# Attention over 4096 positions in split fp32: moving three SBUF tiles by 64 bytes and widening two row pitches from 258 to 260 floats

## The chip, the cores and the metric

The kernel runs on one core of one Trainium2 chip. The metric is device time in microseconds (us) of one execution, taken as the median of several runs. A core has a matrix engine (PE in the profile, with its weight loads shown apart as PEld), a vector engine (DVE), an activation engine (ACT), GpSimd (POOL) and SyncE (SP). They work from an on-chip memory of 128 partitions (SBUF), and PE writes to accumulators (PSUM). A matmul multiplies a stationary operand, which a weight load (LDWEIGHTS) brings into the array, with a moving operand, which the MATMUL streams through it. Both are read from SBUF.

## The reference

For each of four images x of shape 64 x 64 x 256, with N = 4096 positions and C = 256 channels, the reference makes q and k (128 wide) and v (256 wide) by projection, an N x N table of energies, its softmax, and the weighted sum of v:

```python
q = x @ Wq + bq ; k = x @ Wk + bk ; v = x @ Wv + bv
pq = q.reshape(B, -1, N); pk = k.reshape(B, -1, N); pv = v.reshape(B, -1, N)
energy = einsum('bcn,bcm->bnm', pq, pk)
attention = softmax(energy, axis=-1)
out = einsum('bcm,bnm->bcn', pv, attention)
out = gamma * out.reshape(x.shape) + x
```

The reshape runs over the flat memory of an image, so "channels" and "positions" of the attention are not those of the convolution layout; the kernel handles that with the way it loads its rows.

## The kernel before

PE multiplies in a fast form of fp32 (fp32r) that drops low bits. To keep accuracy, every factor is held in three forms: h (an upper part), l and d (two combinations of the rest with the upper part). A product then takes three matmuls. This holds for the energies (forms of q and k side by side in the tiles `q` and `k`) and for the weighted sum (tiles `h`, `l`, `d` of the exponentials against `vh`, `vl`, `vd` of v).

`vh` and `vl` are [128 partitions, 32 blocks m, 258 floats]: 256 of v and two columns of ones (L208), so that the sum of the exponentials falls out of the same matmul. `vd` is [128, 32, 256]. The three stay in SBUF for a whole image. `h`, `l` and `d` are [128, 4, 256] each, in pools with three, two and two buffers.

An image first goes through 16 projection rounds (transposes L123, `qk` L136, `v` L157, then the forms are made on ACT and DVE). Then come 128 steps u, eight (t = 0 to 7) for each of 16 groups g of 256 output rows, so 512 steps over four images. In one step PE does this, in the order the program gives by hand:

- `energy` (L303): 12 matmuls for the step three ahead. Stationary is a 128 x 128 slice of `k`, moving a 256-wide slice of `q`. ACT takes the exponentials (L307) and DVE multiplies their two halves (`join`, L317).
- `attend` (L351), called for j = 0 and 1: 12 matmuls each, four with `vh` and `h`, four with `vl` and `l`, four with `vd` and `d`. Stationary is `left[:, i, n]`, 512 bytes for each partition; moving is row m of `vh`, `vl` or `vd`, with m = 2t + i//2 + 16*(i%2). So i = 0 and 1 read rows with even m, i = 2 and 3 rows with odd m.

DVE makes `l` (L328) and `d` (L331) one step ahead. At the end of a group `whole` and `finish` scale, transpose (`ot`, L389), add x and write the output with a DMA from POOL's queue (L394).

After the last image a check runs: `ok`, a [128, 128] tile in the pool `const`, is made on DVE from the row sums `zall` (L474 to L476), reduced to `zs` (L477), summed over partitions by a matmul (`zp`, L480), and cast to `again` (L481). All engines load `again` and branch on it (L488); a general version of the kernel follows behind that branch and does not run with this data.

SBUF is given out in the order of the pools: `const`, then `xpool` (x tiles), `xtpool`, `qkv` (the v forms), `ppool` (x, y, h, l, d), `work`, `kpool`.

Of the kernel before, what the change touches and what calls it, by code (L numbers as in the profile page):

```python
# [9 lines left out]
F32 = mybir.dt.float32  # L10
F32R = mybir.dt.float32r
I32 = mybir.dt.int32
AF = mybir.ActivationFunctionType
ALU = mybir.AluOpType
AX = mybir.AxisListType
# [5 lines left out]
def kernel(  # L21
# [36 lines left out]
    nc = tc.nc  # L58
    B, W, H, C = x.shape
    P = 128  # L60
    N = W * H
    C2 = C // 2
    NM = N // P
    KC = C // P
    NI = NM // 2
    Z_LOW, Z_HIGH = 2.0**-60, 2.0**80
# [11 lines left out]
    const = ctx.enter_context(tc.tile_pool(name="const", bufs=1))  # L78
# [8 lines left out]
    ones = const.tile([P, P], F32, name="ones")  # L87
# [87 lines left out]
    NJ = NB // P  # L175
    NG = N // NB
    NU = NM // 4
    STEPS = NG * NU
    LOOK = 3
    E = 2.0**-12  # L180


# [5 lines left out]
    bv4_sb = const.tile([P, KC], F32, name="bv4_sb")  # L188
    nc.scalar.mul(bv4_sb, bv_sb, 1.0 / E)

    with ExitStack() as fast:
        fast.enter_context(tc.manual_schedule())
        pool = lambda name, bufs, **kw: fast.enter_context(
            tc.tile_pool(name=name, bufs=bufs, **kw)
        )
        xpool, xtpool, qkv = pool("xpool", 3), pool("xtpool", 3), pool("qkv", 1)
        ppool, work, kpool = pool("ppool", 2), pool("work", 2), pool("kpool", 3)
        dram = pool("dram", 2, space=DRAM)
        ps_s = pool("ps_s", 2, space=PSUM)
# [1 line left out]
        ps_t = pool("ps_t", 1, space=PSUM)  # L201


        vh = qkv.tile([P, NM, C + 2], F32R, tag="vh", name="vh")
        vl = qkv.tile([P, NM, C + 2], F32R, tag="vl", name="vl")
        vd = qkv.tile([P, NM, C], F32R, tag="vd", name="vd")
        for t in (vh, vl):
            nc.vector.tensor_copy(t[:, :, C:], ones[:, : 2 * NM].rearrange("p (m t) -> p m t", t=2))  # L208

        images, qd, kf, units, loads, now = [], {}, {}, {}, {}, {}  # L210

# [13 lines left out]
        def image(b):  # L225
# [7 lines left out]
            def v_out(i):  # L233
                now["v4"] = work.tile([P, KC, C], F32, tag="v4", name=f"v4_{b}_{i}")
                return now["v4"], bv4_sb, 1.0 / E

# [7 lines left out]
        def halved(f, x):  # L244

            h = f[:, :, 0, :]
            nc.scalar.activation(h, x, AF.Identity, scale=UPPER / 64)  # L247
            for j, s, op in ((1, -64.0, ALU.add), (2, 64.0 * (1.0 + E), ALU.subtract)):
                nc.vector.scalar_tensor_tensor(
# [12 lines left out]
        def project_v(b, i):  # L262
# [3 lines left out]
            h = vh[:, m, :C]  # L266
            nc.scalar.activation(h, v4, AF.Identity, scale=UPPER * E)  # L267

            for t, f in ((vl, 1.0 / E), (vd, 1.0 / E + 1.0)):
                nc.vector.scalar_tensor_tensor(  # L270
# [19 lines left out]
        def energy(b, u, k):  # L290
# [10 lines left out]
            for i in range(2):  # L301
                for to, f, first, last in ((sa, 0, True, False), (sa, 1, False, True), (sb, 2, True, True)):
                    nc.tensor.matmul(  # L303
                        to[:, i], kt[:, 2 * k + i, f, :], q[:, :, f, :], start=first, stop=last
                    )
            for to, sp, scale in ((x, sa, (1.0 + E) / E), (y, sb, -1.0 / E)):
                nc.scalar.activation(  # L307
# [28 lines left out]
        def attend(b, u, j):  # L336
            g, t = divmod(u, NU)
            if t == j == 0:
                now["acc"] = [
                    ps_o.tile([P, C + 2], F32, tag=f"a{j}", name=f"a{j}_{b}_{g}")  # L340
                    for j in range(NJ)
                ]
                now["bb"] = ps_o.tile([P, NJ, C], F32, tag="bb", name=f"bb_{b}_{g}")
            h, l, d = units[b, u]
            a, bb = now["acc"][j], now["bb"]
            n = slice(j * P, (j + 1) * P)
            for out_, left, right in ((a, h, vh), (a, l, vl), (bb[:, j, :], d, vd)):
                for i in range(4):
                    m = 2 * t + i // 2 + NI * (i % 2)

                    nc.tensor.matmul(  # L351
                        out_,
                        left[:, i, n],
                        right[:, m, :],
                        start=(t == i == 0 and (left is h or left is d and j == 0)),
                        stop=(t == NU - 1 and i == 3 and left is not h),
                        skip_group_check=True,
                    )
            if t == NU - 1 and j == NJ - 1:
                now["o"] = work.tile([P, NJ, C], F32, tag="o", name=f"o_{b}_{g}")  # L360
                nc.scalar.copy(now["o"], bb)
# [51 lines left out]
        for b in range(B):  # L413
# [17 lines left out]
            for u in range(STEPS):  # L431
                g, t = divmod(u, NU)
                ahead = u + LOOK
                if ahead // NU + 1 < NG and ahead % NU == 3:
# [23 lines left out]
                for j in range(NJ):  # L458
                    attend(b, u, j)
# [10 lines left out]

    zs = const.tile([P, 1], F32, name="zs")
    zf = zall.rearrange("p n j -> p (n j)")
    ok = const.tile([P, B * NG * NJ], F32, name="ok")
    nc.vector.tensor_scalar(ok, zf, Z_LOW, None, ALU.is_ge)  # L474
    nc.vector.scalar_tensor_tensor(ok, zf, Z_HIGH, ok, ALU.is_le, ALU.mult)
    nc.vector.tensor_reduce(zs, ok, AX.X, ALU.min)  # L476
    nc.vector.tensor_scalar(zs, zs, 0.5, None, ALU.is_lt)  # L477
    with tc.tile_pool(name="ps_z", bufs=1, space=PSUM) as ps_z:
        zp = ps_z.tile([P, 1], F32, name="zp")
# [4 lines left out]
    NG = N // NB  # L484
    NJ = NB // P
    NP = NM // 2
    xg, og = columns(x, NB), columns(out, NB)
    with tc.If(nc.values_load(again[0:1, 0:1]) > 0), ExitStack() as general:  # L488
        pool = lambda name, bufs, **kw: general.enter_context(
            tc.tile_pool(name=name, bufs=bufs, **kw)  # L490
        )
        xpool, xtpool, qkv = pool("gx", 2), pool("gxt", 2), pool("gqkv", 1)
# [4 lines left out]
        for b in range(B):  # L497
# [16 lines left out]
            for g in range(NG):  # L514
                ps = []
                mx = work.tile([P, 2, NB], F32, tag="mx", name=f"gmx_{b}_{g}")
                for t in range(NP):
# [9 lines left out]
                    p = ppool.tile([P, 2, NB], F32, tag="p", name=f"gp_{b}_{g}_{t}")  # L527
# [89 lines left out]
```

## Time and profile before

| what | value |
|---|---|
| median of 4 runs | 2520.83 us (2519.0 to 2521.51) |
| the profiled execution's own time | 2522.84 us |
| its span, first to last instruction | 2520.7 us |
| granted TensorE clock, mean over the span | 0.997 |
| busy share PE / PEld / DVE / ACT / POOL | 99% / 97% / 83% / 72% / 17% |
| matmuls L351 (`vh`, `vl`, `vd`), each | 4096 of 285, 283, 281 ns |
| matmuls L303 (`sa`, `sb`) | 4096 of 280 ns, 2048 of 281 ns |
| `x`, `l`, `d` on DVE, 512 each | 1222, 1219, 1219 ns |
| mean rate of DMA | 198 GB/s |

Matmuls overlap in the array, so the mean duration of one (some 280 ns) is not what it costs. What counts is the step from the start of one to the start of the next, which a timeline shows.

### The profile page before, as it was taken

How to read it: one execution, taken by the hardware profiler on the slowest of the kernel's cores; microseconds unless marked ns; L12 is line 12 of the kernel's file. 1: busy time of each engine (PE TensorE's matmuls, PEld its weight loads, DVE VectorE, ACT ScalarE, POOL GpSimd, SP SyncE). 2: the span in 40 equal slices, each digit the busy share in tenths (PEclk: the TensorE clock that was granted, in tenths of full speed). 3: DMA queues.
4: the chain of work that ended last, by engine and by line, in shares of the span. 5: the costliest groups of instructions: out<-in, count | busy, mean ns of one | idle time of the engine just before them, and what ended most of it. 6: DMA issues, size and time to landing. Idle time of an engine off the chain costs nothing.

```text
span 2520.7 us, 49987 instructions
## 1 busy us (share of the span) xinstructions
PE 2486.9 (99%) x19970; PEld 2440.3 (97%) x19970; DVE 2103.8 (83%) x2440; ACT 1805.4 (72%) x3138; POOL 424.8 (17%) x774
## 2 busy tenths in 40 slices
PE   8999999999999999999999999999999999999998
PEld 7999999999899999999989999999998999999998
DVE  4888888888688888888868888888876888888886
ACT  4777777777577777777667777777766777777775
POOL 3211111111311111111041111111114111111110
PEclk9999999999999999999999999999999999999999
DMA  6666666664766666656476666666547666666663
GB/s 213 207 209 198 206 196 194 207 206 155 223 211 193 209 199 207 199 190 208 141 240 211 199 195 209 200 206 197 190 148 235 210 207 192 205 200 206 199 198 98
DMA packets 137967, 498.92 MB, mean 198 GB/s; under 512 B 15872, under 2 KB 57856, under 8 KB 137728
## 3 DMA queue, kind: packets, MB, share of 16 engines
q0 software_dynamic: 92160, 453.03, 56.0%
q1 hardware_dynamic: 44032, 41.96, 5.5%
q8 instruction: 160, 2.62, 0.4%
q10 hardware_dynamic: 1536, 0.66, 0.1%
q14 instruction: 79, 0.65, 0.1%
HBM read 445.25 MB, written 50.33 MB: 197 GB/s over the span
## 4 chain that ended last, share of the span: by engine, by line
PE 90%; issue 3%; ACT 3%; DVE 2%; DMA 1%; POOL 0%; POOLq 0%; ACTq 0%; DVEq 0%
PE a L351 38%; PE bb L351 19%; PE sa L303 18%; PE sb L303 10%; PE qk L136 2%; PE v L157 1%; ACT v L166 1%; DMA k<-kf 1%; PE ot L389 1%; ACT vh L267 1%; DVE qks L145 1%; ACT f L247 1%; DVE vd L270 0%; PE xt L123 0%; DMA bv_sb<-in_L_conv_bv_dram 0%
## 5 line engine op out<-in xcount | busy, mean ns | idle before, releaser
L307 ACT ACTIVATE x<-sa 128x512 f32<-128x512 f32 x1024 | 608.3, 594 | 430.7 <-PE sa L303 421.4
L317 DVE TENSOR_TENSOR x<-x,y 128x1024 f32<-128x1024 f32 x512 | 625.7, 1222 | 164.9 <-ACT y L307 164.9
L303 PE MATMUL sa<-q,k 128*128 128x256 f32 x4096 | 744.7, 280 | 9.1 <-DMA k<-kf 5.1
L351 PE MATMUL a<-vh,h 128*128 128x258 f32 x4096 | 666.7, 285 | 0.0
L351 PE MATMUL a<-vl,l 128*128 128x258 f32 x4096 | 659.7, 283 | 1.7 <-DVE l L328 1.7
L351 PE MATMUL bb<-vd,d 128*128 128x256 f32 x4096 | 650.7, 281 | 1.8 <-DVE d L331 1.8
L303 PEld LDWEIGHTS sa<-q,k 128*128 128x128 f32 x4096 | 623.0, 189 | 11.3 <-ACT x L307 5.0
L331 DVE SCALAR_TENSOR_TENSOR d<-h,x 128x1024 fp32r<-128x1024 f32 x512 | 624.0, 1219 | 0.0
L328 DVE TENSOR_TENSOR l<-x,h 128x1024 fp32r<-128x1024 f32 x512 | 624.0, 1219 | 0.0
L307 ACT ACTIVATE y<-sb 128x512 f32<-128x512 f32 x1024 | 612.5, 598 | 0.0
L303 PE MATMUL sb<-q,k 128*128 128x256 f32 x2048 | 576.4, 281 | 0.0
L351 PEld LDWEIGHTS a<-vl,l 128*128 128x128 f32 x4096 | 563.1, 189 | 2.6 <-DVE l L328 2.6
L322 ACT ACTIVATE h<-x 128x1024 fp32r<-128x1024 f32 x512 | 543.4, 1061 | 29.4 <-DVE x L317 29.4
L351 PEld LDWEIGHTS a<-vh,h 128*128 128x128 f32 x4096 | 560.4, 190 | 1.3
L351 PEld LDWEIGHTS bb<-vd,d 128*128 128x128 f32 x4096 | 556.5, 188 | 2.6 <-issue 2.0
L287 POOL DMA_DIRECT2D k<-kf x512 | 283.3, 554 | 1487.1 <-PE sb L303 1467.0
L303 PEld LDWEIGHTS sb<-q,k 128*128 128x128 f32 x2048 | 384.5, 188 | 8.5 <-ACT y L307 1.0
L136 PE MATMUL qk<-wqk_sb,xts 128*128 128x256 f32 x512 | 124.6, 387 | 5.1 <-ACT xts L129 5.1
L157 PE MATMUL v<-xts,wv_sb 128*128 128x256 f32 x512 | 120.3, 379 | 0.0
L381 ACT ACTIVATE o<-o,r 128x256 f32<-128x256 f32 x128 | 58.4, 504 | 74.0 <-DVE r L379 74.0
L157 PEld LDWEIGHTS v<-xts,wv_sb 128*128 128x128 f32 x512 | 97.4, 190 | 13.3
L136 PEld LDWEIGHTS qk<-wqk_sb,xts 128*128 128x128 f32 x512 | 94.6, 195 | 16.2 <-ACT xts L129 5.5
(41 smaller groups left out, 876.7 us busy)
## 6 DMA issues: line engine op xcount, KB each, us to landing
k<-kf POOLq DMA_DIRECT2D x512, 768.0 KB, 4.7
x<-in_x_dram SPq DMA_DIRECT2D x128, 256.0 KB, 3.3
kf<-f POOLq DMA_DIRECT2D x64, 384.0 KB, 3.7
out_dram<-x POOLq DMA_DIRECT2D x64, 256.0 KB, 2.5
qd<-qks POOLq DMA_DIRECT2D x128, 64.0 KB, 2.2
qr<-qd SPq DMA_DIRECT2D x64, 128.0 KB, 3.1
wv_sb<-in_L_conv_Wv_dram ACTq DMA_DIRECT2D x1, 256.0 KB, 4.2
wqk_sb<-in_L_conv_Wq_dram ACTq DMA_DIRECT2D x1, 128.0 KB, 2.1
```

What stands on the lines that cost most here:

```text
L136: nc.tensor.matmul(qk[:, s, :], self.xt[i][:, k, s, :], wqk_sb[:, k, :], start=(k == 0), stop=(k == KC - 1),)
L145: nc.vector.tensor_tensor(dst, qk[:, :, o : o + w], bqk_sb[:, o : o + w].unsqueeze(1).to_broadcast([P, 2, w]), ALU.add,)
L157: nc.tensor.matmul(vp[:, eh, :], wv_sb[:, k, eh * P : (eh + 1) * P], self.xt[i][:, k].rearrange("p s a -> p (s a)"), start=(k == 0), stop= ...
L287: nc.gpsimd.dma_start(t.rearrange("p (i s) f d -> p i s (f d)", s=2), kf[b, u % NU])
L303: nc.tensor.matmul(to[:, i], kt[:, 2 * k + i, f, :], q[:, :, f, :], start=first, stop=last)
L307: nc.scalar.activation(to[:, 2 * k : 2 * k + 2, :], sp.rearrange("p i j d -> p i (j d)"), AF.Exp, scale=scale,)
L317: nc.vector.tensor_tensor(x, x, y, ALU.mult)
L322: nc.scalar.activation(h, units[b, u], AF.Identity, scale=UPPER)
L328: nc.vector.tensor_tensor(l, x, h.bitcast(F32), ALU.subtract)
L331: nc.vector.scalar_tensor_tensor(d, h.bitcast(F32), 1.0 + E, x, ALU.mult, ALU.subtract)
L351: nc.tensor.matmul(out_, left[:, i, n], right[:, m, :], start=(t == i == 0 and (left is h or left is d and j == 0)), stop=(t == NU - 1 and ...
L381: nc.scalar.activation(o[:, j, :], o[:, j, :], AF.Identity, scale=r[:, j : j + 1])
```

## The change

The tile `pad` of [128, 16] floats (64 bytes for each partition) is allocated behind `qkv` and never used. The rows of `vh` and `vl` are VC = 260 floats apart (1040 bytes) where they were 258 (1032 bytes); the ones still fill columns 256 and 257, and the matmul reads as many columns as its output has (258). To make room, `ok` leaves `const` for a pool `check` that is opened after the main pools are closed, and so lies where x tiles lay.

```diff
+    VC = C + 4
...
         xpool, xtpool, qkv = pool("xpool", 3), pool("xtpool", 3), pool("qkv", 1)
+
+        pool("pad", 1).tile([P, 16], F32, name="pad")
         ppool, work, kpool = pool("ppool", 2), pool("work", 2), pool("kpool", 3)
...
-        vh = qkv.tile([P, NM, C + 2], F32R, tag="vh", name="vh")
-        vl = qkv.tile([P, NM, C + 2], F32R, tag="vl", name="vl")
+        vh = qkv.tile([P, NM, VC], F32R, tag="vh", name="vh")
+        vl = qkv.tile([P, NM, VC], F32R, tag="vl", name="vl")
...
-            nc.vector.tensor_copy(t[:, :, C:], ones[:, : 2 * NM].rearrange("p (m t) -> p m t", t=2))
+            nc.vector.tensor_copy(t[:, :, C : C + 2], ones[:, : 2 * NM].rearrange("p (m t) -> p m t", t=2))
...
-                        right[:, m, :],
+                        right[:, m, : out_.shape[1]],
...
-    ok = const.tile([P, B * NG * NJ], F32, name="ok")
-    nc.vector.tensor_scalar(ok, zf, Z_LOW, None, ALU.is_ge)
-    nc.vector.scalar_tensor_tensor(ok, zf, Z_HIGH, ok, ALU.is_le, ALU.mult)
-    nc.vector.tensor_reduce(zs, ok, AX.X, ALU.min)
+    with tc.tile_pool(name="check", bufs=1) as check:
+        ok = check.tile([P, B * NG * NJ], F32, name="ok")
+        nc.vector.tensor_scalar(ok, zf, Z_LOW, None, ALU.is_ge)
+        nc.vector.scalar_tensor_tensor(ok, zf, Z_HIGH, ok, ALU.is_le, ALU.mult)
+        nc.vector.tensor_reduce(zs, ok, AX.X, ALU.min)
```

Where the tiles lie (byte address in a partition, first buffer) in the two built programs:

| tile | before | after |
|---|---|---|
| `vh`, first row | 36128 | 35616 |
| `vl`, first row | 69152 | 68896 |
| `vd`, first row | 102176 | 102176 |
| `h` / `l` / `d` | 155424 / 167712 / 175904 | 155488 / 167776 / 175968 |
| `q` / `k` | 194336 / 210784 | 194400 / 210848 |
| `ok` | 23328 | 23328, the first 512 bytes of an x buffer |
| end of the last tile | 229216 | 229280 |

## The prediction

> **What bounds the kernel now.** I read the shares of the page first, then the chain of waits, then the timeline of single steps.
>
> ```profile
> PE 2486.9 (99%) x19970; PEld 2440.3 (97%) x19970; DVE 2103.8 (83%) x2440; ACT 1805.4 (72%) x3138; POOL 424.8 (17%) x774
> ...
> PE a L351 38%; PE bb L351 19%; PE sa L303 18%; PE sb L303 10%; PE qk L136 2%; PE v L157 1%; ACT v L166 1%; DMA k<-kf 1%; PE ot L389 1%; ACT vh L267 1%; DVE qks L145 1%; ACT f L247 1%; DVE vd L270 0%; PE xt L123 0%; DMA bv_sb<-in_L_conv_bv_dram 0%
> ```
>
> PE is never free, and 85% of the chain is L351 and L303. So the end is set by how fast matmuls follow each other. The timeline of PE in the middle of the run shows that, step by step (start, length, engine and line, tiles):
>
> ```profile
> 1002.02 0.39 PE L303 MATMUL sa<-q,k 128*128 128x256 f32 x2
> ...
> 1003.38 0.64 PE L351 MATMUL a<-vh,h 128*128 128x258 f32 x4
> 1003.85 0.64 PE L351 MATMUL a<-vl,l 128*128 128x258 f32 x4
> 1004.33 0.64 PE L351 MATMUL bb<-vd,d 128*128 128x256 f32 x4
> 1004.81 0.64 PE L351 MATMUL a<-vh,h 128*128 128x258 f32 x4
> 1005.29 0.64 PE L351 MATMUL a<-vl,l 128*128 128x258 f32 x4
> 1005.77 0.64 PE L351 MATMUL bb<-vd,d 128*128 128x256 f32 x4
> 1006.25 0.40 PE L303 MATMUL sa<-q,k 128*128 128x256 f32 x2
> ...
> 1028.18 0.40 PE L303 MATMUL sa<-q,k 128*128 128x256 f32 x2
> ...
> 1029.59 0.66 PE L351 MATMUL a<-vh,h 128*128 128x258 f32 x4
> ```
>
> The reader is to see three speeds. Twelve energies take 1003.38 - 1002.02 = 1.36 us, 113.3 ns each; 24 attend matmuls take 1006.25 - 1003.38 = 2.87 us, 119.6 ns each; and in another step twelve energies take 1029.59 - 1028.18 = 1.41 us, 117.5 ns each. Nobody is waited for in any of them. From the start times of all matmuls in the trace I took the step to the next start, leaving out steps over 150 ns: energies have two values and little between, 60% near 113.4 ns and 40% near 117.7, mean 115.3. The others are, on rows of even m and of odd m: `vh` 119.9 and 121.9, `vl` 119.4 and 121.0, `vd` 117.5 and 118.5 ns. Two more columns explain 0.8 ns of the first two (256 columns at 113.4 ns is 0.44 ns each). A step repeats to 1 ns from group to group, so the cause isn't a chance meeting with another engine; it lies in PE's own two reads, whose addresses repeat.
>
> The sum closes: 12288 attend steps at 120.9, 120.2 and 118.0 are 1471 us; 6144 energies at 115.3 are 708; 1024 projection matmuls at 216 and 512 transposes at 109 are 277; steps over 150 ns add 39; the time before the first matmul of line 136 is 11.6, the end after the last of line 351 some 12.6. That is 2519 of the span of 2520.7. The execution's own time, 2522.84, is 2.1 over the span and 2.0 over the median of the runs, so I take differences off the median.
>
> The end of the program matters too:
>
> ```profile
> 2508.00 0.23 DVE L474 TENSOR_SCALAR ok<-zall 128x128 f32<-128x128 f32 x1
> ...
> 2509.72 0.14 DVE L481 CAST again<-zp 128x1 int32<-128x1 f32 x1
> ...
> 2512.82 0.70 POOL L394 DMA_DIRECT2D out_dram<-x  x1 [26.31 <-DVE x L393]
> ```
>
> The check of the row sums is done (2509.86) before the last output leaves (2512.82).
>
> **The change part by part.** *d against vd.* The distance of `d` from `vd` goes from 73728 bytes, a multiple of 128, to 73792, which leaves 64. All rows of `vd` and slices of `d` are multiples of 512 apart, so every one of the 4096 pairs of `bb` changes alike. The trace has one pair of operands that already lies 64 apart: `k` from `q` is 16448 bytes, which leaves 64 by 128, also after the change. It runs at 115.3 ns, `bb` at 118.0. From below: the shift does nothing, 0 us. From above: every `bb` falls to the faster energy value, 4096 x (118.0 - 113.4) = 19 us. I take the energies' mean, as theirs is the nearest row: 4096 x 2.7 = 11 us gained. A loss can't be excluded: all at the slowest kind of step (121.9 less two columns, 121.0) would cost 12 us.
>
> *Rows of vh and vl.* At 1032 bytes rows of odd m begin 8 bytes off a multiple of 16, and the distance to `h` and `l` runs through 8m by 128; at 1040 every row begins on a multiple of 16 and the distance is 64 - 16m. Odd rows are slower by 2.0 (`vh`) and 1.6 ns (`vl`); but `vd`, whose rows are all aligned, has 1.0 for the same places in the program. Taking all of it away gains 2048 x (2.0 + 1.6) = 7.3 us, taking what is over `vd` 2048 x 1.6 = 3.3. I take 7. The 64 bytes do less here: in the trace of before the even rows already sit at distances 0, 16, ... 112 as t goes from 0 to 7, and `vh` reads 119.4, 119.6, 122.1, 120.0, 119.6, 119.5, 119.8, 119.0 ns: nothing good about 64 (t = 4). Ends: every pair at the faster energy value plus two columns (114.2) gains 4096 x (120.9 - 114.2) + 4096 x (120.2 - 114.2) = 52 us; all at the worst of these places (122.1) loses 4096 x (1.2 + 1.9) = 13.
>
> *The energies.* Their distances stay. Which of two values they run at depends on what ran before, since the same tiles give both. All fast gains 6144 x 0.4 x 4.3 = 10.6 us, all slow loses 16. I take 0.
>
> These steps of 113.4 to 121.9 ns, with a pattern that repeats by row at a granted clock of 0.997, are what all three gains rest on. The Trainium skill speaks against them: "TensorE: Matmul & The Clock Gate", Part 2, "Step-by-step: what each phase is for", says that weights and moving operand come through two independent read ports, so that loading the next weights takes nothing from the running matmul. By that page no address matters and the sum would hold the end alone, 2526 us as an estimate. Rows that differ by address under one instruction contradict it, and I go by the rows.
>
> *The check at the end.* `ok` moves into memory of the x tiles, so its first instruction waits until the pool is free, which is when the last output DMA has landed; in the built order it stands behind that output's addition (L393 before). Queued behind it are `zs`, `zp`, `again`, and the load and branch of all five engines. Before, these were hidden under `finish`. The DMA's end is seen at 2516.14 in the trace; from `ok` to `again` is 2509.86 - 2508.00 = 1.86 us; so `again` comes at 2518.0. Before, POOL's load began at 2512.81, and its closing drain ran from 2513.54 for 6.35 us, the last long piece. If it lasts as long again, everything moves by 2518.0 - 2512.8 = 5.2 us. If it was mostly waiting for the DMA, PE's branch (3.69 us in the trace) is next: 2518.0 + 0.6 + 3.7 + 0.9 = 2523.2, 2.5 us late. I take 5, the drain being the row itself.
>
> *Free.* `pad` has no instruction. The ones are as many elements. DVE and ACT keep their counts; DVE needs 3 x 1.22 = 3.66 us of a step of 4.26, so PE could lose 0.6 us of a step (300 us in all) before DVE became the bound.
>
> Sum: -11 - 7 + 0 + 5 = -13, so 2520.8 - 13 = 2508 us.
>
> **The rivals.** *The big gain:* the reads of weights and moving rows collide because both began on the same 128-byte offset, and the steady 113.4 of the energies is what a shifted pair gives. Then `bb` gains 19 and `vh`, `vl` half or all of 52: 2520.8 - 19 - 26 + 5 = 2481, down to 2455. For it: energies hold the low value over twelve matmuls in a row, `bb` never does. Against: distance 64 shows nothing in `vh`.
>
> *Nothing but the rows and the end:* the shift is empty, and 118 for `bb` comes from accumulating in one place or from the order. Then -7 + 5, 2519 us, no change. For it: `vh` by distance; energies have 117.7 too.
>
> *Slower:* a step of the array depends on the state that the step before left, as the two values of the energies show. The new pattern of rows leaves the energies at the slow value from their first matmul on, all through a group: +16 us, the end +5, rows -7: 2535. It decides once the rows give less than 16 + 5. With no gain and no loss in the array the end alone gives 2526.
>
> *It doesn't do what it says:* the addresses of the built program show the shift, so I give this nothing.
>
> **How the numbers follow.** A difference under 0.2% (5 us, 2515.8 to 2525.8) can't be told from none. Forecast (gain in `bb` and rows, less the end): 0.42, its own range 2498 to 2515. Big gain: 0.20. Rows and end alone: 0.15. Slower: 0.23, half of it near 2526. The range 2478 to 2530 leaves out the deep part of the big gain and the full slow energies, about 2 in 10. Faster 0.62, same 0.15, slower 0.23.
>
> **What would show it.** In the profile after: 24 attend matmuls in about 2.82 us where they took 2.87; `bb` steps near 115 ns with the energies' two values; odd and even rows of `vh` alike. `ok` on DVE after the last output DMA, and some 5 us more between the last matmul of the weighted sum and the end. I am wrong if `bb` stays at 118, if the energies change their mix, or if the end is no longer than before.

## The result, and the profile after

The changed kernel takes 2523.04 us (median of 40 runs, 2521.2 to 2524.96), the kernel before 2520.36 us in the same comparison (60 runs). The ratio is 1.0011, 95% interval 1.0007 to 1.0016: slower by 2.7 us, less than the 0.2% that the prediction called no change, and on the other side of the forecast of 2508.

The first lines of the page are nearly those of before. Line numbers have moved by 3: L306 is `energy`, L354 `attend`.

```profile
PE 2483.7 (99%) x19970; PEld 2436.8 (97%) x19970; DVE 2104.1 (83%) x2440; ACT 1811.2 (72%) x3138; POOL 426.4 (17%) x774
...
L354 PE MATMUL a<-vl,l 128*128 128x258 f32 x4096 | 659.3, 283 | 1.7 <-DVE l L331 1.7
L354 PE MATMUL a<-vh,h 128*128 128x258 f32 x4096 | 659.9, 283 | 0.0
L354 PE MATMUL bb<-vd,d 128*128 128x256 f32 x4096 | 649.0, 280 | 1.9 <-DVE d L334 1.9
```

PE still sets the end. `vh` has lost 2 ns of mean duration (285 before), `bb` one (281), `vl` none. The timeline of PE in the same part of the run (start, length, engine and line, tiles) shows what follows from it:

```profile
1005.72 0.40 PE L306 MATMUL sa<-q,k 128*128 128x256 f32 x2
...
1007.12 0.64 PE L354 MATMUL a<-vh,h 128*128 128x258 f32 x4
1007.59 0.65 PE L354 MATMUL a<-vl,l 128*128 128x258 f32 x4
1008.07 0.64 PE L354 MATMUL bb<-vd,d 128*128 128x256 f32 x4
1008.55 0.64 PE L354 MATMUL a<-vh,h 128*128 128x258 f32 x4
...
1009.98 0.40 PE L306 MATMUL sa<-q,k 128*128 128x256 f32 x2
```

24 attend matmuls take 1009.98 - 1007.12 = 2.86 us, 119.2 ns each; the twelve energies ahead of them take 1.40 us, 116.7 each, between the two values of before. Over the whole trace, with the measure of the prediction (from the start of a matmul to the next start, steps over 150 ns left out):

| step, ns | before | after | times | us |
|---|---|---|---|---|
| `vh`, rows of even m | 119.90 | 120.05 | 2048 | +0.3 |
| `vh`, rows of odd m | 121.87 | 118.54 | 2048 | -6.8 |
| `vl`, rows of even m | 119.44 | 120.39 | 2048 | +1.9 |
| `vl`, rows of odd m | 121.04 | 119.99 | 2048 | -2.2 |
| `bb` (`vd`) | 118.02 | 117.74 | 4096 | -1.1 |
| energies | 115.34 | 116.24 | 6144 | +5.5 |
| share of energies at the slow value | 40% | 58% | | |

That is -2.4 us in the array. The last matmul of line 351 started at 2507.96 us before; its like now starts at 2504.04, so the trace is ahead by 3.9 us there. The other 1.5 us lie outside these rows, in the projection rounds (steps of `qk` -1.7, waits ahead of the transposes of x -1.3) and in the energies' steps over 150 ns (+1.3); one profiled execution of each kernel can't tell whether the change has any part in them. Then comes the end:

```profile
2503.80 0.52 PE L354 MATMUL bb<-vd,d 128*128 128x256 f32 x3
...
2508.62 0.70 POOL L397 DMA_DIRECT2D out_dram<-x  x1 [25.89 <-DVE x L396]
2511.26 0.23 DVE L478 TENSOR_SCALAR ok<-zall 128x128 f32<-128x128 f32 x1 [2.94 <-DMA out_dram<-x]
...
2513.06 0.16 DVE L485 CAST again<-zp 128x1 int32<-128x1 f32 x1 [0.74 <-PE zp L484]
```

`ok` waits 2.94 us for the last output to land, and `again` is ready at 2513.22, 4.6 us behind the issue of that output, where it was 3 us ahead of it before. From the start of the last `bb` to the end of the span it is 17.13 us, before 12.76: +4.4 us. Together -2.4 + 4.4 = +2.0, against the 2.7 of the medians. The span grew by 0.5 us only, thanks to that 1.5 us; the profiled execution of the kernel before took 2522.84 us, 2.5 over the median here, that of the changed kernel 2523.29, 0.3 over. The steps themselves repeat better than that: e1 and e4 below give those of before and of after again to 0.1 ns by kind.

So three things need an explanation: why `bb` did not gain from the 64 bytes, why the energies got slower though their distance is the same, and what the rows did.

### The profile page after: what moved, and what is told of

It is laid out like the page before. It is cut to its first block, busy times and chain, and to the rows that moved or that the text cites. A ratio compares the mean times of both kernels' runs of the same rounds, so it can differ in the third digit from the quotient of the medians.

```text
span 2521.2 us, 49989 instructions
## 1 busy us (share of the span) xinstructions
PE 2483.7 (99%) x19970; PEld 2436.8 (97%) x19970; DVE 2104.1 (83%) x2440; ACT 1811.2 (72%) x3138; POOL 426.4 (17%) x774
## 4 chain that ended last, share of the span: by engine, by line
PE 91%; ACT 3%; DVE 3%; issue 2%; DMA 1%; POOL 0%; DVEq 0%; POOLq 0%; ACTq 0%
PE a L354 39%; PE bb L354 19%; PE sa L306 19%; PE sb L306 10%; PE qk L136 2%; PE v L157 1%; ACT v L166 1%; PE ot L392 1%; ACT vh L270 1%; DVE qks L145 1%; DMA k<-kf 1%; DVE vd L273 1%; ACT f L250 1%; PE xt L123 0%; DMA bv_sb<-in_L_conv_bv_dram 0%
## 5 line engine op out<-in xcount | busy, mean ns | idle before, releaser
L306 PE MATMUL sa<-q,k 128*128 128x256 f32 x4096 | 750.4, 281 | 8.0 <-ACT x L310 4.0
L354 PE MATMUL a<-vl,l 128*128 128x258 f32 x4096 | 659.3, 283 | 1.7 <-DVE l L331 1.7
L354 PE MATMUL a<-vh,h 128*128 128x258 f32 x4096 | 659.9, 283 | 0.0
L354 PE MATMUL bb<-vd,d 128*128 128x256 f32 x4096 | 649.0, 280 | 1.9 <-DVE d L334 1.9
L306 PEld LDWEIGHTS sa<-q,k 128*128 128x128 f32 x4096 | 626.1, 189 | 10.2 <-ACT x L310 5.0
L306 PE MATMUL sb<-q,k 128*128 128x256 f32 x2048 | 578.1, 282 | 0.0
L354 PEld LDWEIGHTS a<-vl,l 128*128 128x128 f32 x4096 | 562.7, 190 | 2.6 <-DVE l L331 2.6
L354 PEld LDWEIGHTS bb<-vd,d 128*128 128x128 f32 x4096 | 557.9, 189 | 2.6 <-issue 2.0
L354 PEld LDWEIGHTS a<-vh,h 128*128 128x128 f32 x4096 | 557.0, 189 | 0.9
L306 PEld LDWEIGHTS sb<-q,k 128*128 128x128 f32 x2048 | 384.9, 188 | 9.9 <-ACT y L310 8.2
```

The source lines that it names most:

```text
L306: nc.tensor.matmul(to[:, i], kt[:, 2 * k + i, f, :], q[:, :, f, :], start=first, stop=last)
L354: nc.tensor.matmul(out_, left[:, i, n], right[:, m, : out_.shape[1]], start=(t == i == 0 and (left is h or left is d and j == 0)), stop=(t ...
```

## The experiments

"Distance" is always the address of the stationary operand less that of the moving one, modulo 128 bytes. All steps in ns, measured as above; the slow share is the share of energy steps nearer to 117.7 than to 113.4 ns; "end" is the time from the start of the last `bb` to the end of the span, in us; the ratio is to the kernel before, with its 95% interval, where there were repeated runs ("one run" marks the others).

| run | `vh` | `vl` | `bb` | energies | slow share | end | time, us | ratio |
|---|---|---|---|---|---|---|---|---|
| before | 120.90 | 120.24 | 118.02 | 115.34 | 0.40 | 12.8 | 2520.4 | |
| after | 119.28 | 120.19 | 117.74 | 116.24 | 0.58 | 17.1 | 2523.0 | 1.0011 (1.0007 to 1.0016) |
| e1_end_only | 120.93 | 120.30 | 118.00 | 115.30 | 0.39 | 17.5 | 2526.4 | 1.0018 (1.0009 to 1.0027) |
| e2_pad_only | 121.08 | 120.06 | 117.29 | 116.57 | 0.68 | 12.6 | 2528.4 | 1.0028 (1.0017 to 1.0039) |
| e3_rows_only | 120.26 | 119.77 | 119.11 | 116.08 | 0.59 | 12.8 | 2523.4 | 1.0008 (0.9999 to 1.0017) |
| e4_change_early_end | 119.30 | 120.21 | 117.70 | 116.20 | 0.58 | 12.5 | 2520.2 | 0.9997 (0.9988 to 1.0006) |
| e5_qk_moved | 120.87 | 119.96 | 118.21 | 115.94 | 0.45 | 12.8 | 2522.1 | one run |
| e6_k_plus32 | 120.56 | 120.55 | 118.46 | 117.81 | | 12.9 | 2534.5 | one run |
| e7_k_plus64 | 120.58 | 120.17 | 117.98 | 118.92 | | 12.9 | 2536.0 | one run |
| e8_k_plus96 | 120.62 | 119.72 | 118.18 | 119.33 | | 12.9 | 2537.2 | one run |
| e9_grouped_after | 119.50 | 119.91 | 116.51 | 116.99 | 0.80 | 13.0 | 2519.6 | 0.9995 (0.9985 to 1.0004) |
| e10_grouped_before | 120.31 | 120.11 | 118.62 | 117.74 | 0.94 | 12.8 | 2538.1 | 1.0068 (1.0051 to 1.0084) |
| e11_vh_rows_1152 | 119.76 | 120.08 | 117.48 | 117.05 | 0.81 | 12.7 | 2527.9 | 1.0029 (1.0017 to 1.0042) |
| e12_256_dist64 | 115.80 | 113.66 | 114.13 | 117.49 | 0.89 | 12.8 | 2476.3 | one run |
| e13_256_dist0 | 119.94 | 119.99 | 119.73 | 117.98 | 0.99 | 12.8 | 2537.4 | one run |
| e14_260_columns | 120.11 | 119.57 | 116.22 | 117.42 | 0.89 | 13.0 | 2521.3 | 1.0002 (0.9992 to 1.0012) |
| e15_qk_pad_grouped | 120.19 | 119.55 | 115.79 | 117.62 | 0.90 | 13.0 | 2520.0 | 0.9995 (0.9986 to 1.0004) |
| e16_256_all64 | 117.24 | 116.10 | 116.47 | 116.48 | 0.65 | 12.8 | 2496.6 | one run |
| e17_qk_pad_order_kept | 118.96 | 119.59 | 116.98 | 117.83 | 0.96 | 12.5 | 2519.9 | 0.9993 (0.9984 to 1.0002) |
| e18_256_order_kept | 115.75 | 113.51 | 113.99 | 117.48 | 0.89 | 12.5 | 2474.5 | one run |

The median of the kernel before was between 2521.3 and 2522.1 us in the comparisons of e1 to e18.

### The parts of the change alone

**e1_end_only**: the kernel before, with `ok` moved as in the change.

```diff
-    ok = const.tile([P, B * NG * NJ], F32, name="ok")
+    with tc.tile_pool(name="check", bufs=1) as check:
+        ok = check.tile([P, B * NG * NJ], F32, name="ok")
...
```

> Only the tile of the last check is moved, as in the change: it lies in memory of the x tiles. The layout of all matmul operands is that of before, moved as a whole by 512 bytes. My theory: the array runs as before (vh 120.9, vl 120.2, bb 118.0, energies 115.3 ns a step), and the end after the last matmul of the weighted sum grows from 12.7 to some 17 us, so the whole is 4 to 5 us over before (ratio 1.0017). Rival (the end's cost lies in the layout, or is hidden by closing work): the whole is within 1 us of before.

The array is that of before to 0.1 ns in every kind, the end is 17.5 us (+4.7), the whole 5.1 us slower by the medians (ratio 1.0018, that is 2 to 7 us). Its timeline has the same order as that of the changed kernel:

```profile
2506.42 0.63 PE L351 MATMUL bb<-vd,d 128*128 128x256 f32 x4
...
2514.34 0.23 DVE L475 TENSOR_SCALAR ok<-zall 128x128 f32<-128x128 f32 x1 [2.93 <-DMA out_dram<-x]
```

The rival falls: moving the tile costs what the end showed, and nothing hides it.

**e2_pad_only**: the kernel before with the tile `pad`, which fits without moving `ok`.

```diff
+        pool("pad", 1).tile([P, 16], F32, name="pad")
```

> Only the 64 bytes are added behind the v forms; rows stay 258 floats apart and the last check stays early. Shift theory (distance of 64 between d and vd helps): bb falls from 118.0 towards 115.3 ns, 5 to 11 us faster. State theory (the shift only gives the array other meeting points, without a direction): bb stays within 1 ns of 118, the energies' share of slow steps moves somewhere from 40%, the whole is within 6 us of before. If the energies' loss in the changed kernel comes from their own addresses (q and k moved by 64), the slow share rises to some 58% here too.

`bb` falls by 0.7 ns, 3 us, and the energies rise by 1.2 ns, 7.6 us, with 68% of them slow. The shift alone costs 0.28%. Both theories missed the size of that loss; the shift theory's 5 to 11 us are not there. The share that the expectation's last sentence foresaw was passed (68% for 58%), but e5 and e3 speak against its reason.

**e3_rows_only**: rows of 260 floats, no pad. The last check works without a tile: the minimum and the maximum of the row sums are compared with the bounds.

```diff
+    VC = C + 4
...
+    nc.vector.tensor_reduce(zs[:, 0:1], zf, AX.X, ALU.min)
+    nc.vector.tensor_reduce(zs[:, 1:2], zf, AX.X, ALU.max)
+    nc.vector.tensor_scalar(zs[:, 0:1], zs[:, 0:1], Z_LOW, None, ALU.is_ge)
+    nc.vector.scalar_tensor_tensor(zs[:, 0:1], zs[:, 1:2], Z_HIGH, zs[:, 0:1], ALU.is_le, ALU.mult)
```

> Only the rows of vh and vl are 260 floats apart; no pad. The last check works with a minimum and a maximum of the row sums and needs no tile, so it stays early. Alignment theory: odd rows of vh fall from 121.9 to about 118.5 ns, and of vl from 121.0 to about 120, 4 to 7 us, and bb stays at 118.0; the whole is 2 to 7 us faster, less what the energies' mix gives or takes. Rival (odd rows gained by the shift, not by the alignment): odd rows of vh stay near 122.

Odd rows of `vh` fall to 120.5 only (118.5 with the pad), odd rows of `vl` to 120.6: `vh` and `vl` give 4.5 us. But `bb` rises by 1.1 ns and the energies by 0.7, though `vd`, `d`, `q` and `k` all lie where they lay before: 4.5 + 4.5 us lost. Here two kinds of matmul lose what their neighbours gain, with no change of their own. Neither theory said so.

**e4_change_early_end**: the change whole, with that form of the last check.

> The changed layout whole (pad and rows), with the last check early, by a minimum and a maximum. My theory: steps as in the changed kernel (vh 119.3, vl 120.2, bb 117.7, energies 116.2), the end back at 12.7 us: 4 to 5 us under the changed kernel, 1 to 3 us under before (ratio 0.9993). Rival (the check costs nothing): as the changed kernel, 2 to 3 us over before.

Every step is that of the changed kernel, and the end is 12.5 us. Here `again` is ready ahead of the last output again:

```profile
2507.11 0.14 DVE L485 CAST again<-zp 128x1 int32<-128x1 f32 x1
...
2510.00 0.70 POOL L397 DMA_DIRECT2D out_dram<-x  x1 [25.91 <-DVE x L396]
```

Its ratio, 0.9997, lies under the changed kernel's 1.0011 and the intervals don't meet; against before it can't be told from no change. So the layout is worth somewhere between 3 us gained and 1.5 lost, and the moved check costs more than the layout gives.

### What sets an energy's step

**e5_qk_moved** puts the 64 bytes behind the tiles of the exponentials, so only q and k move, together.

```diff
-        ppool, work, kpool = pool("ppool", 2), pool("work", 2), pool("kpool", 3)
+        ppool = pool("ppool", 2)
+        pool("pad", 1).tile([P, 16], F32, name="pad")
+        work, kpool = pool("work", 2), pool("kpool", 3)
```

> The 64 bytes of the change lie behind the tiles of the exponentials instead of ahead of them: q and k move by 64 together, everything that the attend matmuls read stays where it was before. State theory (which of its two values an energy takes is left behind by the attend matmuls ahead of it, and not set by its own addresses): the energies stay at 115.3 ns with 40% slow, attend steps as before, the array's sum within 2 us of 2218. Rival (q's and k's own place makes the energies of the changed kernel slower): slow share near 58%, energies at 116.2 ns.

A share of 45% (115.9 ns) is nearer to the 40% of before than to the 58% and 68% of the runs in which `h`, `l` and `d` moved, though the array's sum rises by some 3 us where the expectation allowed 2. But the mean hides that the energies are slow at other places than before: in the steps t = 1, 5 and 7 of a group, where it was t = 2 and 3. Attend pairs and energy pairs have kept their distances; what has changed is the border, the first k against the last row of `vd` and the first `h` against the last q. In e3 nothing of q and k moved and the share was 59%. So the energies' own addresses don't set the value alone; what runs ahead has a part in it. Whether the border has is asked further down.

**e6_k_plus32, e7_k_plus64, e8_k_plus96** move k alone, by a pad of 8, 16 or 24 floats ahead of `kpool` (shown for e6). Then an energy's distance is 96, 0 or 32 instead of 64.

```diff
+        pool("pad", 1).tile([P, 8], F32, name="pad")
         kpool = pool("kpool", 3)
```

> k alone moves by 32 bytes: its distance from q goes from 64 to 96 (by 128); attend operands stay. Energies run twelve in a row at one distance, so their steady values show what a distance does. Distance theory: one steady value that depends on it, lower than 113.4 or higher than 117.7 ns somewhere among the three distances 96, 0 and 32. State theory: two steady values again at every distance, only the share changes.

> k alone moves by 64 bytes: distance 0 from q, which is the distance that d had from vd before. Distance theory: energies rise to the 118 of bb before. State theory: two values near 113.4 and 117.7 again, share anywhere.

> k alone moves by 96 bytes: distance 32 from q. Distance theory: a steady value of its own, as said for a distance of 96. State theory: two values near 113.4 and 117.7 again, share anywhere.

The distance theory holds in the mean: 117.8 ns at 96, 118.9 at 0, 119.3 at 32, against 115.3 at 64. Its steady value doesn't appear, nor do the two values of the state theory: steps spread from 112 to 127 ns. Distance 32 is no better than 0, so that equal offsets are the bad case is not shown. Twelve energies of e7:

```profile
1005.88 0.40 PE L305 MATMUL sa<-q,k 128*128 128x256 f32 x2
...
1007.30 0.64 PE L353 MATMUL a<-vh,h 128*128 128x258 f32 x4
```

1.42 us, 118.3 ns each, where the fast step of before had 1.36. So the kernel before already had its energies at the best of the four distances, and the reading in the prediction that 64 is a good distance was right. Then why not for `bb`?

### Why bb gained nothing

**e9_grouped_after and e10_grouped_before** give `attend` another order: both j for `vh`, both for `vl`, both for `vd`, so each kind runs eight in a row. e9 has the change's layout with the early check, e10 the layout of before.

```diff
-            for out_, left, right in ((a, h, vh), (a, l, vl), (bb[:, j, :], d, vd)):
-                for i in range(4):
+            for kind, left, right in ((0, h, vh), (0, l, vl), (1, d, vd)):
+                for j in range(NJ):
+                    out_ = bb[:, j, :] if kind else acc[j]
...
+                    for i in range(4):
```

> Layout of the change, last check early, and the attend matmuls of a step in another order: vh for j = 0 and 1, then vl for both, then vd for both, so that d against vd (distance 64) runs eight in a row and stands ahead of the energies (distance 64 as well). Theory: distance 64 is good, as the energies of the runs with k moved show (115.3 ns at 64 against 117.8 to 119.3 elsewhere), but a run of four is too short to reach its steady value. Then bb falls from 117.7 to 114 to 116 and the energies' slow share falls, 10 to 25 us under before. Rival (distance does nothing for bb since it accumulates in one place): bb stays within 0.7 of 117.7, the whole within 5 us of e4.

> The order of e9 on the layout of before: d at distance 0 from vd, rows 258. Theory: bb stays at 117 to 119 over eight in a row, as the energies did at distance 0 (118.9); the whole within 6 us of before. Rival (long runs alone are what helps): bb falls as in e9.

In e9 `bb` is 116.5, in e10 118.6. The timelines of e9, two `bb` of eight and the energy behind each, and of e10, one:

```profile
1007.48 1.07 PE L355 MATMUL bb<-vd,d 128*128 128x256 f32 x8
1008.39 0.40 PE L306 MATMUL sa<-q,k 128*128 128x256 f32 x2
...
1011.72 1.10 PE L355 MATMUL bb<-vd,d 128*128 128x256 f32 x8
1012.67 0.40 PE L306 MATMUL sa<-q,k 128*128 128x256 f32 x2
```

```profile
1007.49 1.11 PE L352 MATMUL bb<-vd,d 128*128 128x256 f32 x8
1008.44 0.40 PE L303 MATMUL sa<-q,k 128*128 128x256 f32 x2
```

At distance 64 eight take 0.91 us (113.8 ns) or, in the next step, 0.95 (118.8); at distance 0 0.95. Step by step the pattern is plainer: at distance 64 `bb` starts anywhere between 113 and 123 ns and, after two to five matmuls, sits at 113.4 or at 117.7, the two values of the energies. In t = 7 of e9, for example, the eight read 123, 116, 114, 113, 113, 113, 113 and 118 ns (medians over the groups; the last leads over to the energies). At distance 0 (e10) it reaches a steady 120 in four of the eight t and settles in none of the others. So the accumulation in one place (e9's rival) is not it.

The changed kernel's runs of four show the same start cut short: in five of the eight t the first four `bb` of a step read 117 to 125, 116, 114 and 113 ns, so they reach the good value with the last one.

As wholes both runs missed what was expected. e9 is only 0.05% under before, inside its interval, where 10 to 25 us were foreseen, since the slow share of its energies rose to 80% instead of falling from 58%. e10 is 17 us over before, where at most 6 were foreseen: its energies are 94% slow (117.7 ns).

**e11_vh_rows_1152** adds rows of 288 floats for `vh`, so that all its pairs have distance 64.

```diff
-        vh = qkv.tile([P, NM, VC], F32R, tag="vh", name="vh")
+        vh = qkv.tile([P, NM, C + 32], F32R, tag="vh", name="vh")
...
-                now["o"] = work.tile([P, NJ, C], F32, tag="o", name=f"o_{b}_{g}")
+                now["o"] = work.tile([P, NJ, C], F32, tag="v4", name=f"o_{b}_{g}")
```

> As e9, and the rows of vh 288 floats apart (1152 bytes, a multiple of 128), so that every pair of h and vh is 64 apart; the o tiles share the buffers of v4 to make room. Distance theory with a period of 128 bytes: vh falls from 119.3 to 114.5 to 117 ns (two columns more than an energy), vl stays near 120, 8 to 20 us under e9. Rival (the period is longer than 128, or the distance matters only for operands like the energies'): vh stays within 1 ns of 119.3.

`vh` stays at 119.8: a constant distance of 64 by 128 isn't enough. Its eight steps are now the same in t = 2, 5 and 6 (122, 128, 113, 119, 122, 116, 121, 119 ns) and, but for the first, in t = 3 and 7. The pattern repeats, it just never settles. The whole is 8 us over e9. Two things still tell `vh` from `bb`: its width of 258, and its rows, 1152 bytes apart, whose distances within a step are equal by 128 but not by 256 or 512 as those of `bb` are. The second is the longer period that the expectation's rival names; this run doesn't exclude it.

**e12_256_dist64 and e13_256_dist0** take the two columns of ones away; the sums of the exponentials are left out and taken as 1. Rows of all three v forms are 1024 bytes apart. e12 has the pad, e13 has not; order as in e9.

```diff
-    VC = C + 4
+    VC = C
...
-            nc.vector.tensor_copy(t[:, :, C : C + 2], ones[:, : 2 * NM].rearrange("p (m t) -> p m t", t=2))
...
-                nc.vector.tensor_copy(zall[:, b * NG + g, j : j + 1], a[:, C : C + 1])
+                nc.vector.tensor_copy(zall[:, b * NG + g, j : j + 1], ones[:, j : j + 1])
```

> vh and vl have no columns of ones: rows of 256 floats, 1024 bytes apart, matmuls 256 wide, the 64 bytes of the pad kept. So every pair of the array, energies included, has 256 columns and distance 64. The sums of the exponentials are left out and taken as 1. Theory (a pair at distance 64 settles to 113.4 or 117.7 ns if nothing disturbs it, and the 258th column, 8 bytes more in each row, is what disturbs it): all of vh, vl and bb hold these two values, mean between 113.4 and 117.7, and 36 matmuls of a step run at one of them. Rival (vh and vl are slow since two matmuls in a row accumulate in place): vh and vl stay near 119.

> As e12 without the pad: distance 0 in all attend pairs, 64 still for the energies. The sums of the exponentials are left out and taken as 1. Theory: vh, vl and bb settle to 120 ns as bb did in e10 with eight in a row; the array is 12288 x 2.3 to 6.6 ns, 28 to 81 us, slower than in e12. Rival (a run without the two columns settles anywhere): as e12 within 10 us.

The timelines of PE, first e12, then e13:

```profile
1002.78 1.09 PE L353 MATMUL a<-vh,h 128*128 128x256 f32 x8
1003.71 1.07 PE L353 MATMUL a<-vl,l 128*128 128x256 f32 x8
1004.61 1.07 PE L353 MATMUL bb<-vd,d 128*128 128x256 f32 x8
1005.52 0.60 PE L391 MATMUL ot<-ident,o 128*128 128x128 f32 x4
```

```profile
1002.68 1.12 PE L352 MATMUL a<-vh,h 128*128 128x256 f32 x8
1003.64 1.12 PE L352 MATMUL a<-vl,l 128*128 128x256 f32 x8
1004.60 1.12 PE L352 MATMUL bb<-vd,d 128*128 128x256 f32 x8
1005.56 0.40 PE L303 MATMUL sa<-q,k 128*128 128x256 f32 x2
```

At distance 64 eight take 0.90 to 0.93 us, 113 to 116 ns each; at distance 0 eight take 0.96 us three times over, 120.0 each. The tile `pad` is the only difference of the two programs. The same 64 bytes that are worth 3 us in the layout of the change (e3 against e4) move this one by 61 us (2537.4 to 2476.3). Against e9, `vh` and `vl` fall from 119.5 and 119.9 ns to 115.8 and 113.7. Two columns less explain 0.8 ns of that by their count; the rest goes to the width and to the row pitch of 1024 bytes, which changed together.

**e14_260_columns** asks whether it is the 8 bytes over a multiple of 16: four columns of ones, matmuls 260 wide, otherwise e9.

```diff
-            nc.vector.tensor_copy(t[:, :, C : C + 2], ones[:, : 2 * NM].rearrange("p (m t) -> p m t", t=2))
+            nc.vector.tensor_copy(t[:, :, C:], ones[:, : 4 * NM].rearrange("p (m t) -> p m t", t=4))
...
-                    ps_o.tile([P, C + 2], F32, tag=f"a{j}", name=f"a{j}_{b}_{g}")
+                    ps_o.tile([P, VC], F32, tag=f"a{j}", name=f"a{j}_{b}_{g}")
```

> As e9, with four columns of ones instead of two and matmuls 260 wide, so that a row read is a multiple of 16 bytes. Theory of the 8 bytes: vh and vl become steadier and lose 1 to 3 ns against 119.5 and 119.9 though the two columns more cost 0.8; the whole up to 15 us under e9. Rival (only a distance that stays the same from row to row settles, and here it moves by 16 bytes a row): vh and vl rise by 0.8 and the whole by 7 us.

`vh` 120.1 (+0.6), `vl` 119.6 (-0.3), the whole 1.7 us over e9: no gain, and less of a loss than the 7 us of the rival. With a distance that moves by 16 bytes a row, a multiple of 16 bytes per read is no help. A width of 260 at a constant distance wasn't tried.

**e18_256_order_kept** tells the neighbours from the run length: the order of the changed kernel, four in a row, but 256 wide (the sums of the exponentials are left out and taken as 1), with the pad and the early check.

> The order of matmuls of the changed kernel (vh, vl, vd for one j, then for the other), its pad, its early form of the last check as in e4, and vh and vl without the columns of ones: 256 wide, rows 1024 bytes apart, so distance 64 in all attend pairs. The sums of the exponentials are left out and taken as 1. If the 258 columns are what kept bb from gaining in the changed kernel, bb falls from 117.7 to a mix of 113.4 and 117.7 though it still runs only four long, and vh and vl do so too: whole between 2470 and 2500 us. If the short runs were the cause, bb stays above 117 and the whole above 2505.

```profile
1007.69 0.64 PE L352 MATMUL a<-vh,h 128*128 128x256 f32 x4
1008.17 0.62 PE L352 MATMUL a<-vl,l 128*128 128x256 f32 x4
1008.62 0.62 PE L352 MATMUL bb<-vd,d 128*128 128x256 f32 x4
1009.08 0.62 PE L352 MATMUL a<-vh,h 128*128 128x256 f32 x4
1009.53 0.62 PE L352 MATMUL a<-vl,l 128*128 128x256 f32 x4
1009.99 0.62 PE L352 MATMUL bb<-vd,d 128*128 128x256 f32 x4
1010.44 0.40 PE L304 MATMUL sa<-q,k 128*128 128x256 f32 x2
```

Four take 0.45 to 0.46 us once `vh`'s first four (0.48) are past: 113 to 114 ns, through all kinds. 2474.5 us. Against e4 the distance of `d` from `vd`, the order and the runs of four are the same, and `bb` falls from 117.7 to 114.0. So short runs are no obstacle by themselves; the neighbours are. In the changed kernel `bb` starts each of its runs of four from the state that `vl` left, and settles late or not at all. Which property of the neighbours it is stays open: e18 takes away their two columns and, with the row pitch, the distance that moves by 16 bytes a row. No run has one without the other.

### What picks one of the two values

**e15_qk_pad_grouped, e16_256_all64, e17_qk_pad_order_kept** put 64 more bytes ahead of q and k, in e9, e12 and e4. Then also the pairs on the borders (first k with the last row of `vd`, first `h` with q) lie at 64 where they lay at 0.

```diff
+        pool("pad2", 1).tile([P, 16], F32, name="pad2")
         work, kpool = pool("work", 2), pool("kpool", 3)
```

> e9 with 64 more bytes ahead of q and k. In e9 the pairs on the border between two kinds lie at distance 0: the first slice of k from the last row of vd, and the first slice of h from q. Now these are 64 apart too; inside every kind nothing changes. Border theory: energies keep the value that bb leaves, so their slow share falls from 0.80 to 0.5 or less, the last of bb from 117 to 113 or 114 ns, 8 to 20 us under e9. Rival (the value is taken anew at each start of a kind): share stays near 0.8, the whole within 5 us of e9.

> e12 with 64 more bytes ahead of q and k: every pair of the 36 in a step is 256 wide and 64 apart, borders too. The sums of the exponentials are left out and taken as 1. Border theory: energies fall from 117.5 to near 113.5, the first of vh from 121 and 122 likewise, everything near 113.5 after the first steps of a group: 6144 x 4 + 4096 x 2 = 33 us under e12, some 2443 us; or, should the slow value be the one that holds, all near 117.7 and some 2515. Rival: as e12 within 8 us.

> The changed layout with the last check early (e4) and 64 more bytes ahead of q and k, order of the matmuls as in the changed kernel. Border theory: bb runs only four long ahead of the energies, so it has not always settled; slow share of the energies between 0.2 and 0.6 (0.58 in e4), 0 to 12 us under e4. Rival: share and whole as e4 within 3 us.

The border theory falls. In e15 `bb` does end at 113 ns in six of eight t, and the energies behind it still go slow, 90% of them:

```profile
1009.31 1.09 PE L357 MATMUL bb<-vd,d 128*128 128x256 f32 x8
1010.23 0.40 PE L308 MATMUL sa<-q,k 128*128 128x256 f32 x2
...
1011.65 1.13 PE L357 MATMUL a<-vh,h 128*128 128x258 f32 x8
```

The twelve energies take 1.42 us, 118.3 each, behind a `bb` of 0.92 for eight. In e17 the share is 96%. In e16 all kinds mix, 2496.6 us, 20 us over e12, neither the 2443 nor the 2515 of the border theory nor within the rival's 8 us of e12. What decides between 113.4 and 117.7 stays open: it changes with anything that runs ahead, repeats from group to group, and none of the theories tried foretold it.

No complete version beats the kernel before beyond its interval; e17 (0.9993), e9, e15 (0.9995) and e4 (0.9997) lie just under it. e12 and e18, at 2476 and 2475 us, leave the sums of the exponentials out; no run here gets these without widening the matmuls, so what a complete kernel would keep of the 46 us isn't known.

## Why the prediction was wrong, point by point

**What bounds the kernel**: right. PE sets the end in all runs, and the steps of the four kinds of matmul with the end give +2.0 us for the difference of the two kernels, where 2.7 were measured.

**d against vd, "4096 x 2.7 = 11 us gained": wrong, 1.1 us measured.** This is the step that failed most, by 10 us; with the energies' 5.5 it turned the sign, which neither would have done alone. The prediction took the energies' mean as the nearest row for a pair at distance 64, as if a pair had a price of its own. The distance itself was read rightly: e6 to e8 show 64 as the best of four, and e13 against e12 a steady 120 against 113.4. What it missed is that the state a run starts from counts: the energies' 115.3 is the mean of runs of twelve alike, while `bb` runs four long behind `vl` and spends most of its run settling. e18 shows the other half: between neighbours of equal width and distance `bb` goes to 114.0, more than was forecast, in the changed kernel's own order. The prediction had a row that pointed there: `vh` at distance 64 (t = 4) was no better than elsewhere. There two such pairs in a row stand between others, yet it used the row against the big gain alone and not against its own 11 us.

**Rows of vh and vl, "I take 7": 6.8 measured** (-6.6 and -0.2), right in sum by luck. Odd rows of `vh` fell by 3.3 ns where 2.0 were foreseen, odd rows of `vl` by 1.0 where it was 1.6, and even rows of `vl` rose by 1.0. With the rows alone (e3) `vh` and `vl` gain 4.5 us and `bb` loses as much. Alignment as such is not shown to be worth anything: the new pitch aligns the row starts and changes the distances at once, and the aligned width of e14 gains nothing over e9.

**The energies, "I take 0": 5.5 us lost.** The prediction had both ends (-10.6 and +16) and the reason, that their value depends on what ran before. e3 shows the reason right: nothing of q and k had moved, and the share rose from 40% to 59%. What could not be had from the trace of before was the direction, and the runs leave it open.

**The check at the end, "I take 5": 4.4 us in the trace, 5.1 in e1.** Right, and by the mechanism given: `ok` starts when the last output has landed, POOL's closing drain takes 6.35 us as before, though that output has landed ahead of it now (2511.3 against 2514.0) and had not before, and everything behind `ok` moves. The 5.2 us of the working counted on a transfer of 3.3 us from issue to landing; in the changed kernel it took 2.5.

**The sum.** -11 - 7 + 0 + 5 became -1.1 - 6.8 + 5.5 + 4.4 = +2.0. Two of the prediction's own signs of being wrong came: `bb` stayed near 118, and the energies changed their mix. By its terms the nearest rival is "nothing but the rows and the end" (2519), with the energies' loss, which the rival "slower" had named at 16 us for a mechanism like the one found, added; by the number alone the 2526 of the end alone is as near. The big gain did not happen. That the distance of the two operands can be worth as much is what e12 and e13 show; that the two reads collide is the argument for it, which no view shows, and equal offsets are not the one bad case (e8).

**The rule of the skill** that the prediction weighed ("TensorE: Matmul & The Clock Gate", Part 2, two independent read ports for weights and moving operand) leaves no room for e12 and e13, most steps of which are 113.4 against 120.0 ns with nothing changed but 64 bytes between the weights and the moving operand; here the measurement decides.

## What to carry to other kernels

Where matmuls follow each other back to back, look at the step from start to start by kind and by place, not at the mean duration: where a pattern repeats to a nanosecond, move one operand by a few bytes and see whether it changes. Here a distance between weights and moving operand paid when all attend matmuls had the same width and distance (61 us between e13 and e12); among neighbours two columns wider, at distances that change from row to row, the same pad gave nothing (e2: 7 us lost). So a price read off one kind of matmul can't be carried to another without asking what runs just ahead of it. And a tile that moves to make room can join a queue it never stood in: ask what must have finished before its new memory is free.

## What the runs showed of the hardware that was not expected

- Back-to-back fp32r matmuls of 256 columns with a new 128 x 128 weight load each settle at one of two steps at distance 64, 113.4 or 117.7 ns, and hold either over a run of eight or twelve (e12). At distance 0 most attend steps of e13 take 120, while energies at distance 0 (e7) don't settle, mean 118.9. Means of the energies at 96 and 32 were 117.8 and 119.3.
- Settling takes two to five matmuls (e9, e18). At 258 columns and rows of 1152 bytes it didn't happen at a distance of 64 (e11: a pattern of eight from 113 to 128 ns).
- The granted clock lay between 0.996 and 0.998 in all profiled executions, far too close together for steps that differ by 5%.
- 64 bytes without any instruction changed the time from 2537 to 2476 us in one kernel, and by 7 us the other way in another.
